# Moving three jobs along the steps of a two-layer banded-mixing kernel: inverse roots, output statistics, group norm

## The chip, the core and the metric

The kernel runs on one core of a Trainium2 chip. A core has a matrix engine (TensorE, PE in the profile; its weight loads are PEld), a vector engine (VectorE, DVE), a scalar engine (ScalarE, ACT), a general engine (GpSimd, POOL) and an engine that only issues transfers (SyncE, SP). Each works through its own list of instructions in order and waits for others by semaphores. The metric is the device time of one execution in microseconds (us); lower is better.

## The reference, cut to what matters

```python
for layer in (0, 1):                    # x: [1, 512, 512, 64] float32
    g  = _gn(x)                         # group norm: 32 groups of 2 channels over the whole picture
    xn = _ln(g, norm_scale, norm_bias)  # over the 64 channels of each pixel
    left  = (xn @ Wl + bl) * mask * sigmoid(xn @ Wlg + blg)    # 128 channels
    right = (xn @ Wr + br) * mask * sigmoid(xn @ Wrg + brg)
    gate  = sigmoid(xn @ Wog + bog)
    out = zeros
    for d in range(-4, 5):              # a band of nine rows
        out[i, j] += left[i, i + d] * right[i + d, j]
    out = _ln(out, out_norm_scale, out_norm_bias) * gate       # over the 128 channels
    x = x + out @ Wo + bo
```

The second layer's group norm needs the sums of the whole first layer, so the layers run one after the other.

## The kernel before

**Tiling.** The 512 rows are cut into nine blocks of 64 rows (they overlap by eight), the columns into two halves of 256 that lie on the two halves of the 128 partitions. A half has two chunks of `JC` = 128 columns, so a layer has 18 chunks; a chunk has `NU` = 16 units of `JU` = 8 columns. All arithmetic is float32.

**Steps.** `layer` runs over steps `t`. In step `t` unit `t` is projected, and output unit `t`, which was projected `LAG` = 30 steps earlier, is finished. So a layer has 288 steps with a projection, and 30 more that only finish outputs. In what follows "step 0" to "step 15" mean `t` modulo 16, and "step 12" is any `t` with that remainder. Instructions are put on each engine's list in the order in which the Python code emits them (`InOrder`), so the position in the loop body is the position in the queue, on SyncE's list too. The helper records every instruction as line 362, which is why the profile's rows all show L362 and have to be told apart by their tiles.

**A unit's way in.** Its pixels come by two DMAs from SyncE (`load`, z). Two steps later `affine` applies the group norm (z<-z,ga and z<-z,gb, on GpSimd; for the first units of a layer on VectorE). A step after that `inner_stats` takes four statistics instructions on VectorE (sti<-z). Every fourth step `solve` turns statistics into inverse roots. Then `inner_norm` (z<-z,sti and z<-z,rs, GpSimd), `transposed` (PE banks<-ident,z) and `kept` (ACT zT, and a DMA to `later`), and in the unit's own step two calls of `right`: PE projects (banks<-pack,zT), ACT takes the sigmoid (sg<-banks), and VectorE multiplies into RO (RO<-banks,sg).

**Mixing.** When the 16 units of a chunk are in RO, steps 0 to 9 of the next 16 run its 16 calls of `mix`, one or two a step (`2, 1, 2, 2, 1, 2, 1, 2, 2, 1`): 32 matmuls (banks<-RO,A), then one copy back to RO by ACT and one by VectorE.

**A unit's way out.** From step 10 on `out_stats` takes statistics of the mixed columns (sto<-RO, 64 instructions a chunk, four a unit). `solve` makes `rs` and `nm` of them. `norm(outs[t + 1])`, at the end of step `t`, is eight ACT instructions (on<-RO,nm,rs). In the next step follow `gates` (ACT gate<-bank), `turned` (PE bank<-ident,on, VectorE ZH<-bank,pack,gate), and `biased` (GpSimd XR<-XR), and one step later `end` (PE bank<-pack,ZH, VectorE XR<-bank,XR and two DMAs) and, in the first layer only, `sums` (PE acc<-XR).

**The inverse roots.** `solve` is five short VectorE instructions for a full set (var<-sti, var<-sto, var<-var, nm<-sto, rs<-var) followed by twelve on GpSimd, from rsqrt<-rs to nm<-nm,rs. Before the change it stands at the end of steps 3, 7, 11 and 15. The `affine` of step `t + 1` (`then_affine`) is put on GpSimd's list just ahead of it. The outputs whose statistics were complete at step 11 are first used by the `norm` at the end of step 13; those of steps 15, 3 and 7 by the `norm` at the end of steps 1, 5 and 9.

**PSUM.** `right`, `transposed` and `mix` share two buffers of two banks (banks); everything else turns in the single banks (bank). A projection can only start when the buffer two uses earlier was emptied.

Of the kernel before, what the change touches and what calls it, by code (L numbers as in the profile page):

```python
# [22 lines left out]
JU = 8  # L23
JQ = 4
NU = JC // JU
# [54 lines left out]
def tile_two_banded_layers(  # L80
# [7 lines left out]
    _, L, _, D = x.shape  # L88
# [326 lines left out]
    def affine(u: Unit, engine):  # L415

        engine.tensor_tensor(u.z, u.z, mid(ga, JU), ALU.mult)
        engine.tensor_tensor(u.z, u.z, mid(gb, JU), ALU.add)
# [57 lines left out]
    def right(u: Unit, q: int, w: dict):  # L476
        pr = projected(u, q, w["right"]).rearrange("p e k h -> p (e k) h")
        sg = wk.tile([P, JQ, H], F32, tag="sg", name="sg", bufs=2)
        en.scalar.activation(sg, pr[:, :, H:], AF.Sigmoid)
        en.vector.tensor_tensor(  # L480
            RO[:, :, u.c + q : u.c + q + JQ, :],
            pr[:, :, :H].rearrange("p j (h t) -> p h j t", t=2),
            sg.rearrange("p j (h t) -> p h j t", t=2), ALU.mult,
        )
# [31 lines left out]
    def take_left(n: int, h: int) -> bass.AP:  # L516


        A = lp.tile([P, S, HA], F32, tag="A", name="A")
        at = n * size + h * slab + WIN * HA  # L520
        for e in range(2):
            en.sync.dma_start(
                A[e * S : (e + 1) * S].rearrange("p i h -> p (i h)"),
                strided(left_of, at, ((S + 2 * WIN) * HA, S), (1, S * HA)),
            )
        return A
# [33 lines left out]
    def out_stats(o: Out, st: bass.AP, k: int):  # L560
        en.vector.bn_stats(
            st[:, k, :],
            RO[:, :, o.c + 2 * k : o.c + 2 * k + 2, :].rearrange("p h j t -> p h t j"),
        )
# [42 lines left out]
    def recall(o: Out):  # L607
        o.t = ztg.tile([P, JU // 2, P], F32, tag="zg", name="zg")
        en.sync.dma_start(o.t, later[o.at])
# [41 lines left out]
    def fetch(src: bass.AP, o: Out, w: dict, n: int):  # L651
        o.n, o.xr = n, XR[n % len(XR)]
        for e in range(2):
            en.sync.dma_start(o.xr[e * S : e * S + o.blk.m, :, 1 : 1 + 2 * D], rows_of(src, o, e))
# [38 lines left out]
    def layer(src: bass.AP, dst: bass.AP, w: dict, stats: bool, then=None):  # L693
        per = LH // JC
        n_chunks = len(blocks) * per
        LAG = NU + 14
        own = NU - JW // JU
        units, outs, lefts, mixes, looks, slabs = {}, {}, {}, {}, {}, {}
        free = NA * [NU - 2]
        for c in range(n_chunks):  # L700
            b, t0 = blocks[c // per], (c + 1) * NU
            for k in range(NU):
                t = c * NU + k
                units[t] = u = Unit(t, blk=b, j=c % per * JC + k * JU)
                j = k * JU if c % 2 == 0 else (JC + k * JU if k < own else JC - JW + (k - own) * JU)
                u.c = j

            for f in range(NU):
                o = outs[c * NU + LAG + f] = Out(
                    b, units[c * NU + (f + own) % NU], c % per * JC + f * JU  # L710
                )
                looks.setdefault(t0 + (8 + f if f > 3 else 10 + f // 2), []).append(o)

            step = [t0 + n for n, k in enumerate((2, 1, 2, 2, 1, 2, 1, 2, 2, 1)) for _ in range(k)]
            for n, t in enumerate(step):
                mixes.setdefault(t, []).append((c, n * HB))

            for h in range(H // HA):
                slabs.setdefault(free[-NA], []).append((c, h))
                free.append(step[(h + 1) * (HA // HB) - 1] + 1)  # L720
        for n in range(0, NEAR * JQ, JU):
            t = 3 + n // JU * 2
            lefts[t] = Unit(t, near=n)
        first_t, last_t = min(outs), max(outs)

        def inputs(t: int) -> list:
            return [d[t] for d in (units, lefts) if t in d]

        loads, affines, inners = {}, {}, {}
        count = [1, 1, 2, 1, 1, 1, 2, 1, 1, 1, 1, 0, 1, 1, 1, 0]
        ahead = {}
        done = -5 - NU
        for t in range(-7 - NU, n_chunks * NU):
            for _ in range(count[t % NU]):
                ahead[done + 7] = t
                done += 1
        for t in range(n_chunks * NU):
            for u in inputs(t):  # L740
                loads.setdefault(ahead[t] - 2, []).append(u)
                affines.setdefault(ahead[t], []).append(u)
                inners.setdefault(ahead[t] + 1, []).append((t, u))

        early = [u for t in sorted(loads) for u in loads[t] if u.near is None and u.at < 7]
        for u in early:
            load(src, u)
        yield
        A, sti, sto, then_affine = {}, {}, None, []
        for t in range(min(loads), last_t + 3):  # L750
            if then and t == max(units) + 2:
                then()
            for u in loads.get(t, []):
                if u not in early:
                    load(src, u)
            if t + 1 in outs:
                fetch(src, outs[t + 1], w, t + 1)
            for c, h in slabs.get(t, []):
                A[c, h] = take_left(c // per, h)
            if t + 2 in outs:  # L760
                recall(outs[t + 2])

            looking = []
            for o in looks.get(t, []):
                if sto is None:
                    sto = sm.tile([P, NB // 2, 6], F32, tag="sto", name="sto"), []
                st, os = sto
                n = len(os) * (JU // 2)
                looking += [(o, st[:, n : n + JU // 2, :], k) for k in range(JU // 2)]
                os.append(o)  # L770

            for v in looking[:3]:
                out_stats(*v)

            for u in affines.pop(t, []):
                affine(u, en.vector if u.at < NU + 4 else en.gpsimd)
            if t % 4 == 3 and t > NU:
                then_affine = affines.pop(t + 1, [])

            todo = []  # L780
            for at, u in inners.get(t, []):
                key = (at + 2) // 4
                if key not in sti:
                    sti[key] = sm.tile([P, 3 * NB // 4, 6], F32, tag="sti", name="sti", bufs=3), []
                st, us = sti[key]
                n = len(us) * (JU // 2)
                u.mean = st[:, n : n + JU // 2, 1::3]
                todo += [(u, st[:, n : n + JU // 2, :], k) for k in range(JU // 2)]
                us.append(u)

            if t in units:
                right(units[t], 0, w)
            for v in looking[3:5]:
                out_stats(*v)
            if t in outs:
                gates(outs[t], w)
            if t in units:
                right(units[t], JQ, w)
            if t in lefts:
                for q in range(0, min(JU, NEAR * JQ - lefts[t].near), JQ):  # L800
                    left(lefts[t], q, w)
            for u in inputs(t + 2):
                inner_norm(u)
            if t in outs:
                turned(outs[t], w)
            for u in inputs(t + 1):
                transposed(u)
                kept(u)
            if t in outs:
                biased(outs[t], w, stats)  # L810
            for v in looking[5:]:
                out_stats(*v)
            for v in todo:
                inner_stats(*v)
            if t - 1 in outs:
                end(dst, outs[t - 1], w)
            if stats and t - 2 in outs:
                sums(outs[t - 2], t - 2 == first_t, t - 2 == last_t)
            if t % 4 == 3:
                st, us = sti.pop((t + 5) // 4, (None, []))  # L820
                so, os = sto or (None, [])
                sto = None
                for u in then_affine:
                    affine(u, en.gpsimd)
                then_affine = []
                if us or os:
                    solve(w, us, os, st, so)
            if t + 1 in outs:
                norm(outs[t + 1])
            for n, (c, h0) in enumerate(mixes.get(t, [])):  # L830
                mix(c, A[c, h0 // HA], h0)
# [129 lines left out]
```

## Time and profile before

| | |
|---|---|
| median of three runs | 5036.04 us (5017.72 to 5038.81) |
| the profiled execution | 5033.71 us, span of its instructions 5031.9 us |
| engines' busy shares of the span | PE 84%, POOL 76%, DVE 77%, ACT 72% |
| mean granted TensorE clock | 0.963 |
| a chunk (16 steps) in the first layer, 1293.7 to 1415.5 | 121.80 us: PE 114.75, POOL 107.15, ACT 99.87, DVE 99.42 busy |
| 1293.7 to 1415.5: granted clock, DMA share | 1.00, 0.72 |

A row of the timeline gives start, duration, engine, line, operation, output<-inputs, shapes and how many instructions were merged; in brackets stands how long the engine had been idle just before and what released it. The row of a stretch gives its length, then for each engine its busy time and the number of instructions, the granted clock (1.00 is full speed), the DMA share and the rate. Four engines are each busy for more than four fifths of a chunk, so a mean tells little; the steps differ in what holds them.

### The profile page before, as it was taken

What the parts mean: (1) busy time and instruction counts of PE and PEld (TensorE: products, weight loads), DVE (VectorE), ACT (ScalarE), POOL (GpSimd) and SP (SyncE); (2) the same over time, 40 slices, a digit from 0 to 9 for tenths busy, and PEclk for the clock granted to TensorE, in tenths of its full rate; (3) what the DMA queues carried; (4) which work ended last, traced back from release to release, by engine and by line L of the source; (5) the groups of instructions that cost most, each with busy time, mean ns of one, the idle gap of its engine ahead of it and who ended that gap; (6) DMA issues with size and microseconds to landing.
All of it is one profiled execution on the core that took longest, in us unless ns stands there. A gap on an engine that the chain in (4) does not pass through costs nothing. (4 is left out here: it accounts for less than half of the span.)

```text
span 5031.9 us, 173294 instructions
## 1 busy us (share of the span) xinstructions
PE 4211.9 (84%) x67090; PEld 3564.2 (71%) x67090; DVE 3875.7 (77%) x9661; ACT 3636.6 (72%) x8156; POOL 3827.9 (76%) x4739
## 2 busy tenths in 40 slices
PE   1026899999999999999984589999999999998998
PEld 0024788888888888888863477777777777777776
DVE  6774778888888888888766478888888888888877
ACT  0013688888888888888883268888888888888888
POOL 0036888888888888888734688888888888888863
PEclk9988999999999999999997899999999999999999
DMA  7914677767776776777663457777777777777766
GB/s 316 406 57 120 172 200 200 204 197 200 203 199 199 198 201 198 198 199 205 190 168 95 118 172 199 203 202 201 199 205 201 202 202 202 204 204 202 206 186 173
DMA packets 905343, 982.32 MB, mean 195 GB/s; under 512 B 114210, under 2 KB 641608, under 8 KB 900168
## 3 DMA queue, kind: packets, MB, share of 16 engines
q1 hardware_dynamic: 897248, 948.49, 65.2%
q10 hardware_dynamic: 7272, 22.73, 1.1%
q8 instruction: 531, 8.70, 0.8%
q14 instruction: 292, 2.39, 0.2%
HBM read 658.42 MB, written 312.46 MB: 193 GB/s over the span
## 5 line engine op out<-in xcount | busy, mean ns | idle before, releaser
L362 ACT ACTIVATE on<-RO,nm,rs 128x128 f32<-128x128 f32 x4608 | 1868.6, 495 | 13.2 <-PE bank L362 12.7
L362 PE MATMUL banks<-pack,zT 64*128 64x256 f32 x9360 | 1322.6, 404 | 128.9 <-ACT zT L362 56.2
L362 PEld LDWEIGHTS banks<-pack,zT 64*128 64x128 f32 x9360 | 884.9, 194 | 493.7 <-DVE RO L362 200.8
L362 PE MATMUL banks<-RO,A 64*64 64x128 f32 x18432 | 1169.4, 279 | 14.4 <-ACT zT L362 14.4
L362 PEld LDWEIGHTS banks<-RO,A 64*64 64x64 f32 x18432 | 1097.4, 184 | 41.3 <-ACT zT L362 17.2
L362 DVE TENSOR_TENSOR RO<-banks,sg 128x512 f32<-128x512 f32 x1152 | 787.8, 684 | 347.6 <-ACT sg L362 331.5
L362 ACT ACTIVATE sg<-banks 128x512 f32<-128x512 f32 (+1 forms) x1188 | 694.7, 587 | 364.1 <-PE banks L362 254.3
L362 DVE COPY RO<-banks 128x512 f32<-128x512 f32 x576 | 397.9, 691 | 592.8 <-ACT RO L362 592.8
L362 DVE BATCH_NORM_STATS2 sto<-RO 128x6 f32<-128x256 f32 x2304 | 847.1, 414 | 1.2
L362 DVE SCALAR_TENSOR_TENSOR ZH<-bank,pack,gate 128x448 f32<-128x448 f32 (+1 forms) x1152 | 738.7, 683 | 51.3 <-ACT gate L362 39.5
L362 POOL TENSOR_TENSOR z<-z,gb 128x512 f32<-128x512 f32 x536 | 686.6, 1281 | 42.0
L362 PE MATMUL bank<-pack,ZH 128*64 128x64 f32 x18432 | 689.4, 230 | 5.6 <-ACT gate L362 5.2
L362 POOL TENSOR_TENSOR z<-z,ga 128x512 f32<-128x512 f32 x536 | 688.5, 1284 | 0.1
L362 POOL TENSOR_TENSOR z<-z,rs 128x512 f32<-128x512 f32 x586 | 616.1, 1051 | 46.0
L362 PEld LDWEIGHTS bank<-pack,ZH 128*64 128x64 f32 x18432 | 608.0, 142 | 47.8 <-ACT gate L362 9.2
L362 POOL TENSOR_TENSOR z<-z,sti 128x512 f32<-128x512 f32 x586 | 623.1, 1063 | 0.0
L362 ACT ACTIVATE gate<-bank 128x448 f32<-128x448 f32 (+1 forms) x1152 | 566.2, 544 | 73.1 <-PE bank L362 63.0
L362 PE MATMUL bank<-zg,pack 64*128 64x448 f32 (+1 forms) x2304 | 551.7, 550 | 1.2 <-DMA zg<-later 0.8
L362 ACT COPY RO<-banks 128x512 f32<-128x512 f32 x576 | 335.7, 583 | 299.2 <-PE banks L362 299.2
L362 PEld LDWEIGHTS bank<-ident,on 64*128 64x128 f32 x9216 | 402.6, 139 | 210.1 <-ACT gate L362 97.2
L362 POOL TENSOR_TENSOR XR<-XR,pack 120x512 f32<-120x512 f32 (+1 forms) x352 | 418.7, 1191 | 135.2 <-DMA XR<-in_x_dram 50.4
L362 PE MATMUL bank<-ident,on 64*128 64x64 f32 x9216 | 443.2, 225 | 86.3 <-ACT gate L362 59.3
(140 smaller groups left out, 3756.7 us busy)
## 6 DMA issues: line engine op xcount, KB each, us to landing
later<-zT SPq DMA_DIRECT2D x576, 256.0 KB
A<-left_of SPq DMA_DIRECT2D x576, 256.0 KB
zg<-later SPq DMA_DIRECT2D x576, 256.0 KB
z<-in_x_dram SPq DMA_DIRECT2D x576, 128.0 KB
z<-mid_x SPq DMA_DIRECT2D x576, 128.0 KB
gn_x<-in_x_dram SPq DMA_DIRECT2D x16, 4096.0 KB
XR<-in_x_dram SPq DMA_DIRECT2D x448, 112.0 KB
mid_x<-XR SPq DMA_DIRECT2D x448, 112.0 KB
```

The lines of the kernel that those rows point to most:

```text
L362: return lambda *a, **k: tc.keep_in_program_order(f(*a, **k))
```

## The change

1. **Inverse roots.** `solve` moves from steps 3, 7, 11, 15 to steps 4, 8, 12, 0 (`t % 4 == 0`), and with it the `affine` put ahead of it (now that of steps 1, 5, 9, 13). The sets are regrouped to fit: `key = (at + 1) // 4`. The step of each `norm` stays.
2. **Output statistics.** They are emitted one by one (an instruction takes two columns of each half) from a list of counts. Before: 8, 8, 4, 4, 4, 4 in steps 10 to 15, 4 in each of steps 0 to 7, none in 8 and 9. After: 5, 5, 6, 3, 3, 3 in steps 10 to 15, 7 in step 0, 4 in each of steps 1 to 8, none in 9. In a step the first three stand ahead of the first RO<-banks,sg, the fourth and fifth ahead of the second, the rest after ZH.
3. **Group norm.** The units handled in steps 0 to 15 were 1, 1, 2, 1, 1, 1, 2, 1, 1, 1, 1, 0, 1, 1, 1, 0 and become 1, 1, 2, 1, 2, 1, 1, 2, 1, 1, 1, 0, 1, 1, 0, 0. A unit's group norm then stands 7 to 10 steps ahead of its projection, where it was 7 to 9. Its two load DMAs stand two steps ahead of it, its statistics one step after it, and both move with it. In steps 0 to 15 of a layer's first chunk one unit is handled in each.

```diff
+        look = [n for n, k in zip(range(10, 25), (5, 5, 6, 3, 3, 3, 7) + 8 * (4,)) for _ in range(k)]
...
-                looks.setdefault(t0 + (8 + f if f > 3 else 10 + f // 2), []).append(o)
+                for k in range(JU // 2):
+                    looks.setdefault(t0 + look[f * (JU // 2) + k], []).append((o, k))
...
-        count = [1, 1, 2, 1, 1, 1, 2, 1, 1, 1, 1, 0, 1, 1, 1, 0]
+        count = [1, 1, 2, 1, 2, 1, 1, 2, 1, 1, 1, 0, 1, 1, 0, 0]
         ahead = {}
-        done = -5 - NU
+        done = -4 - NU
         for t in range(-7 - NU, n_chunks * NU):
-            for _ in range(count[t % NU]):
+            for _ in range(1 if 0 <= t < NU else count[t % NU]):
...
-            if t % 4 == 3 and t > NU:
+            if t % 4 == 0 and t > NU:
                 then_affine = affines.pop(t + 1, [])
...
-                key = (at + 2) // 4
+                key = (at + 1) // 4
...
-            if t % 4 == 3:
-                st, us = sti.pop((t + 5) // 4, (None, []))
+            if t % 4 == 0:
+                st, us = sti.pop((t + 4) // 4, (None, []))
```

No instruction is added or taken away; only their places in the queues change.

## The prediction

> **What bounds the kernel now.** I read the page first (PE 84%, no engine a clear bound), then the stretches of one chunk, then the timeline of each engine through one chunk of the first layer (1293 to 1500 us), because a chunk repeats almost exactly. Taking the first RO<-banks,sg of each step as its start, the median steps 0 to 15 over fourteen chunks last, in the first layer, 10.33, 7.16, 8.96, 8.97, 7.17, 8.97, 7.17, 8.44, 8.87, 7.72, 6.37, 7.01, 5.55, 5.69, 5.68, 8.81 us (122 in all); the second layer's steps differ by a few tenths and make 120.8.
>
> ```profile
> PE 4211.9 (84%) x67090; PEld 3564.2 (71%) x67090; DVE 3875.7 (77%) x9661; ACT 3636.6 (72%) x8156; POOL 3827.9 (76%) x4739
> ...
> 1411.20:1416.30 5.10, 1.86 (x26) 1.29 (x22) 5.07 (x11) 2.45 (x6) 4.50 (x7) 0.98 0.87 261
> 1416.30:1419.70 3.40, 3.37 (x58) 3.21 (x58) 2.67 (x5) 2.64 (x7) 2.80 (x9) 0.52 0.70 214
> 1425.90:1433.10 7.20, 7.20 (x128) 6.34 (x125) 5.89 (x16) 6.39 (x16) 6.96 (x7) 1.00 0.61 172
> ```
>
> The last row is a step 1: PE is busy for all of its 7.20 us. Steps 1 to 9 are PE's, and nothing in this change can shorten them. The first two rows are the seam at the end of step 15: PE works 1.86 of 5.10 us while DVE works 5.07, and afterwards the granted clock is 0.52 for 3.4 us.
>
> ```profile
> 1388.20 0.20 DVE L362 SCALAR_TENSOR_TENSOR var<-sto,pack 128x32 f32<-128x32 f32 x1
> 1388.65 0.20 DVE L362 TENSOR_SCALAR rs<-var 128x64 int32<-128x64 int32 x1
> ...
> 1411.18 0.72 DVE L362 TENSOR_SCALAR var<-sti 128x32 f32<-128x32 f32 x1
> 1411.82 1.31 DVE L362 SCALAR_TENSOR_TENSOR var<-sto,pack 128x32 f32<-128x32 f32 x1
> 1413.26 1.25 DVE L362 TENSOR_SCALAR nm<-sto 128x32 f32<-128x32 f32 x1
> 1415.52 0.67 DVE L362 TENSOR_TENSOR RO<-banks,sg 128x512 f32<-128x512 f32 x1
> ```
>
> ```profile
> 1416.33 0.69 PE L362 MATMUL banks<-ident,z 64*128 64x64 f32 x8 [2.83 <-POOL rsqrt L362]
> 1416.95 1.97 PE L362 MATMUL bank<-pack,ZH 128*64 128x64 f32 x32
> ...
> 1427.09 1.15 PE L362 MATMUL bank<-pack,ZH 128*64 128x64 f32 x32
> ```
>
> ```profile
> 1417.06 0.60 ACT L362 ACTIVATE zT<-banks 128x512 f32<-128x512 f32 x1 [3.41 <-PE banks L362]
> ```
>
> The five DVE instructions of `solve` take 0.73 us at step 11 and 3.4 at step 15 (1411.18 to 1414.61), where GpSimd's group norm runs. So the RO of step 0 starts at 1415.52, PE's transposes wait for that buffer (the profile names rsqrt, but it is RO at 1415.52 plus 0.67 that ends at 1416.19), and ACT stands 3.41 us. Steps 10 and 11 are DVE's: eight statistics of 0.33 us each. Steps 13 and 14 are ACT's, 5.69 us without a gap over 0.15.
>
> **The change part by part.** *Statistics, steps 10 to 12.* DVE's step at 10 is RO, RO, ZH x2, XR (2.95), 4 inner statistics (0.79) and 8 times 0.33: 6.37. With 5 it is 5.4, below ACT's 5.69. Steps 10, 11, 12 become 5.55, 5.69, 5.69 for 18.93: −2.0 us a chunk (second layer the same). The four statistics that go to step 8 lie in PE's time, as those of step 7 do now: 0; without that cover 1.3.
>
> *Roots out of step 15.* DVE then has 2.95 plus three statistics, 3.95, and the step is ACT's: 8.81 becomes 5.69, −3.1 (second layer 8.46 to 5.6, −2.9). *Step 0* keeps PE warm: ZH 1.97 to 1.15, acc 1.02 to 0.64, the z transposes 0.69 to 0.46. From 10.35 it comes to PE's 9.1, −1.25 (second layer 9.97 to 8.6, −1.4). DVE carries there seven statistics, no inner ones, and `solve`: done at RO+5.15, while the copies of `mix` come at RO+5.75, so it is covered by 0.6 us; what goes beyond that is PE's loss.
>
> *The new wait.* The `norm` of step 13 used roots of step 11; now it uses those of step 12.
>
> ```profile
> 1388.93 0.29 POOL L362 TENSOR_TENSOR rsqrt<-rs 128x64 f32<-128x64 f32 x1 [5.75 <-DVE rs L362]
> 1393.26 0.25 POOL L362 TENSOR_TENSOR nm<-nm,rs 128x32 f32<-128x32 f32 x1
> ...
> 1395.30 0.69 DVE L362 TENSOR_TENSOR RO<-banks,sg 128x512 f32<-128x512 f32 x1 [1.19 <-ACT sg L362]
> 1397.24 3.24 ACT L362 ACTIVATE on<-RO,nm,rs 128x128 f32<-128x128 f32 x8
> ```
>
> The twelve GpSimd instructions take 4.6 us (1388.93 to 1393.51), and `norm` starts 1.94 us after RO of step 13. After: DVE reaches `solve` at RO12+4.05 (2.95 and the three statistics that stand between), 0.73 for it, 4.6: roots at RO12+9.4. ACT wants them at 5.69+1.94 = 7.63. ACT stands 1.8 us, and behind it in its queue are the sigmoids that release RO of step 14, in ACT's own stretch: all of it counts.
>
> Is GpSimd free at that moment? A unit's group norm takes 2.63, its inner norm 2.13, XR 1.14. From the roots of step 8 (RO8+10.5) to those of 12 its list is 20.97: ready at RO8+31.5, DVE at RO8+31.55. They meet. Here a rule speaks against the change: the Trainium skill, "SBUF — State Buffer", section "SBUF: two separate sides", says that a DVE instruction in a two-port mode or with two SBUF inputs and a GpSimd instruction exclude each other for a whole instruction. The rows agree at step 15 (1.31 and 1.25, each as long as a group norm instruction) but show 0.20 at step 11, where GpSimd had run out of work. By the rule with full overlap I would add 2.7 at each such meeting, by the row of step 11 nothing; since the list ends just there, I take 0.2. The clock is the second place. PE would stand 0.44+2.0 = 2.45 us in step 13. "TensorE: Matmul & The Clock Gate", section "What's actually happening", gives about 3.4 us of idle time before the clock halves, so by it nothing. The trace has the half clock after 2.83, and after four gaps near 2.5 us twice. I take half of the 0.6 us by which slow transposes would delay zT: 0.3. Step 13: +2.3 (+2.6 in the second layer, where GpSimd comes 0.5 later). Between the ends 1.8 and 5.1.
>
> *Step 5.* Roots of step 4, not 3. From the roots of step 0 (RO0+9.8) GpSimd has 28.84 us of work, two group norms now in step 4: RO0+38.6, against DVE at 38.55. Roots at RO4+10.0.
>
> ```profile
> 1459.97 3.27 ACT L362 ACTIVATE on<-RO,nm,rs 128x128 f32<-128x128 f32 x8
> 1463.10 0.62 ACT L362 COPY RO<-banks 128x512 f32<-128x512 f32 x1
> ```
>
> That `norm` starts at RO4+8.99 (RO4 at 1450.98): 1.0 late, and the `mix` copy follows it without a gap, on whose buffer PE waits with 0.35 to spare: +0.65. In the second layer steps 0 to 3 are shorter, GpSimd is 1.0 late, `norm` 2.0: +2.0. *Steps 1 and 9:* roots of step 0 at RO0+9.8, wanted at 10.9: nothing; of step 8 at RO8+10.5, wanted at 10.6 (first layer) and 10.2 (second): +0.1 and +0.3. Before, these had 6 to 9 us to spare.
>
> *Group norm.* Same count; 16 in 16 steps. Its load DMAs move with it on SyncE (two a unit of about 0.55 us issue each). A load 12 steps ahead takes the buffer of the unit transposed the step before, behind whose zT store SyncE stands anyway: 0, and up to 1 us if not.
>
> *The tails.* In the 30 last steps of a layer ACT paces 4.03 us a step.
>
> ```profile
> 4967.62 1.01 ACT L362 ACTIVATE gate<-bank 128x480 f32<-128x480 f32 x2
> 4970.97 0.18 DVE L362 TENSOR_SCALAR rs<-var 128x32 int32<-128x32 int32 x1
> 4972.54 3.27 ACT L362 ACTIVATE on<-RO,nm,rs 128x128 f32<-128x128 f32 x8
> 4974.91 0.25 POOL L362 TENSOR_TENSOR nm<-nm,rs 128x32 f32<-128x32 f32 x1
> ```
>
> From the gate at 4967.62 to roots at 4975.16 are 7.55 us; the next step's `norm` comes after 4.92. A root one step later thus costs 2.65 at each of steps 12, 0, 4, 8, a little more with seven statistics, less where DVE held steps 10 and 11 before. About +13 in the last tail; +9 in the first, where a step takes 4.56. The start: the first roots wait for three more group norms and a set of statistics on DVE (about 5 us), against fewer loads bunched in step 0: +5 in all, between −10 and +15.
>
> Sum a chunk: first layer −2.0−3.1−1.25+2.3+0.65+0.1 = −3.3; second −2.0−2.9−1.4+2.6+2.0+0.3 = −1.4. Times 17 passes: −56 and −24; tails +22, start +5: −53. Against the profiled 5033.7: 4981. The median of the runs shown lies 2.3 above that execution, so 4983.
>
> **The rivals.** *A, GpSimd is behind at the meetings (slower).* Mechanism: at steps 4 and 12 DVE finds GpSimd still in its group norm, its five instructions take 3.4 instead of 0.73, and ACT's `norm` of steps 5 and 13 stands that much longer. For it: the list ends within 0.1 us of DVE in my working, and of a period of 119 us GpSimd has 113 of work plus 0.8 at four hand-overs. Against: the margin at steps 0 and 8 is over 1 us. Price: 4 us a chunk beyond what is counted, 34 passes, +136: 5119. It decides from 1.6 us a chunk on (53/34); below that the gain survives. *B, no measurable change:* the waits of `norm` eat the gain, with a cold PE at step 13 (0.6) and 2 us at step 5 in both layers: about 1.5 us a chunk more, 5034. *C, the wait at step 13 stays hidden:* then the first three terms alone count, −6.35 a chunk times 34, plus 27: 4847. For it, ACT could start late for another reason; against it, 9.4 against 7.63 with rows for both. *That the regrouping does nothing* I exclude: the places in the queues do change.
>
> **How the numbers follow.** About 0.5% (25 us) is what a measurement of this kernel can tell from no change. Likeliest case 0.44, its own range 4945 to 5020, of which 0.04 lies above 5011; C 0.10; B 0.22; A 0.24. Faster 0.50, same 0.26, slower 0.24. The range 4900 to 5105 leaves out most of C and the upper part of A.
>
> **What would show it.** Right: `solve` on DVE near 0.8 us at step 0; step 15 near 5.7 and step 0 near 9.1; the half clock gone from step 0; step 10 and 11 below 5.8; a new wait of ACT's on for POOL nm of about 2 us at step 13 and of 1 to 2 at step 5; in the tails waits of 2 to 3 us every fourth step. Wrong: on without a wait at step 13 (C); DVE's var and nm rows of 1.2 us at steps 4, 12 or 0 and PE gaps above 3 us (A).

## The result: 1.4% faster, and the profile after

| | before | after |
|---|---|---|
| median, run side by side | 5033.94 us (4 runs, 5017.72 to 5038.81) | 4959.99 us (4 runs, 4958.54 to 4963.24) |
| ratio | | 0.9856, 95% interval 0.9839 to 0.9874 |
| profiled execution | 5033.71 us, span 5031.9 us | 4958.54 us, span 4956.7 us |

The forecast was 4983 us with a range of 4900 to 5105. The time fell inside it, 23 us below the point.

From the page of the kernel before, the row of `norm` in the list of groups; then from the page of the kernel after, the engines' row and the row of `norm` (at its end: idle time of ACT ahead of it, and the releaser of most of it).

```profile
L362 ACT ACTIVATE on<-RO,nm,rs 128x128 f32<-128x128 f32 x4608 | 1868.6, 495 | 13.2 <-PE bank L362 12.7
```

```profile
PE 4181.7 (84%) x67090; PEld 3541.9 (71%) x67090; DVE 3844.0 (78%) x9661; ACT 3642.7 (73%) x8156; POOL 3820.6 (77%) x4739
...
L362 ACT ACTIVATE on<-RO,nm,rs 128x128 f32<-128x128 f32 x4608 | 1871.7, 495 | 128.4 <-POOL nm L362 108.4
```

The engines' row says nothing new: the counts are the same and the shares hardly move. The row of `norm` does. The releaser POOL nm does not occur in it before; now ACT loses 108.4 us to it. The change bought time and paid part of it back here.

**Where the time came from.** The step lengths are taken as in the prediction (first RO<-banks,sg of each step, medians over the fourteen chunks 4 to 17):

| step | 0 | 4 | 5 | 6 | 7 | 8 | 10 | 11 | 12 | 13 | 14 | 15 |
|---|---|---|---|---|---|---|---|---|---|---|---|---|
| layer 1 before | 10.33 | 7.17 | 8.97 | 7.17 | 8.44 | 8.87 | 6.37 | 7.01 | 5.55 | 5.69 | 5.68 | 8.81 |
| layer 1 after | 9.09 | 7.17 | 8.97 | 7.58 | 8.96 | 8.44 | 5.55 | 5.69 | 5.68 | 7.50 | 5.94 | 5.75 |
| layer 2 before | 9.97 | 7.49 | 8.50 | 7.26 | 8.19 | 8.51 | 6.37 | 7.02 | 5.56 | 5.88 | 5.57 | 8.46 |
| layer 2 after | 8.51 | 7.72 | 9.55 | 7.58 | 8.49 | 8.47 | 5.55 | 5.58 | 5.74 | 7.50 | 5.63 | 5.76 |

Steps 1 to 3 and 9 differ by 0.06 us at most. The layers divide like this (the tail runs from the first RO of step 287 to the last XR<-bank,XR of the layer; what lies ahead of a layer's first step is not in the table):

| stretch, us | layer 1 before | after | layer 2 before | after |
|---|---|---|---|---|
| first chunk | 149.7 | 131.4 | 146.2 | 130.0 |
| second chunk | 103.8 | 101.5 | 103.3 | 101.3 |
| chunks 3 to 17 together | 1833.1 | 1790.8 | 1811.4 | 1780.1 |
| last chunk (15 steps) | 111.9 | 113.3 | 110.4 | 111.7 |
| tail | 166.9 | 182.2 | 146.1 | 158.8 |

So 34.5 us come from the two first chunks and 73.6 from chunks 3 to 17 of both layers; the tails take back 28.0. With the second chunks (−4.3), the last chunks (+2.7) and what lies ahead of each layer's first step (+6.6), the sum is −75.1, against −75.2 between the spans. Where the text below speaks of a steady chunk, it is the mean of chunks 4 to 17.

**The seam is gone.** The row of each stretch: step 15, step 0 and step 1 of the same chunk as in the prediction. The columns are those of the stretches shown before: length, then busy time and number of instructions of PE, PEld, DVE, ACT and POOL, then the granted clock.

```profile
1376.40:1382.16 5.76, 5.31 (x95) 4.29 (x92) 4.15 (x8) 5.61 (x15) 5.05 (x5) 1.00 0.68 181
1382.16:1391.20 9.04, 8.60 (x154) 7.83 (x155) 7.30 (x19) 7.03 (x16) 6.83 (x13) 1.00 0.78 240
1391.20:1398.40 7.20, 7.20 (x128) 6.34 (x126) 5.88 (x15) 6.39 (x15) 6.89 (x9) 1.00 0.85 230
```

Where PE had worked 1.86 of 5.10 us at the end of step 15, it now works 5.31 of 5.76, and step 0 runs at full clock. The timeline of DVE in that step 0, then of PE:

```profile
1382.16 0.69 DVE L362 TENSOR_TENSOR RO<-banks,sg 128x512 f32<-128x512 f32 x1 [0.89 <-ACT sg L362]
...
1386.54 0.17 DVE L362 TENSOR_SCALAR var<-sti 128x32 f32<-128x32 f32 x1
1386.62 0.19 DVE L362 SCALAR_TENSOR_TENSOR var<-sto,pack 128x32 f32<-128x32 f32 x1
...
1387.06 0.20 DVE L362 TENSOR_SCALAR rs<-var 128x64 int32<-128x64 int32 x1
1387.86 0.69 DVE L362 COPY RO<-banks 128x512 f32<-128x512 f32 x1 [0.60 <-ACT RO L362]
```

```profile
1383.10 0.46 PE L362 MATMUL banks<-ident,z 64*128 64x64 f32 x8
1383.49 1.15 PE L362 MATMUL bank<-pack,ZH 128*64 128x64 f32 x32
```

`solve` takes 0.72 us (1386.54 to 1387.26) instead of 3.4, at RO+4.38, and 0.60 us of slack follow it, as worked out. PE's transposes take 0.46 and ZH 1.15, no longer 0.69 and 1.97.

**The new wait.** Steps 12 and 13 of the same chunk, each engine's timeline in turn. The first RO of step 12 is at 1357.62, that of step 13 at 1363.30.

```profile
1361.67 0.17 DVE L362 TENSOR_SCALAR var<-sti 128x32 f32<-128x32 f32 x1
...
1362.20 0.20 DVE L362 TENSOR_SCALAR rs<-var 128x64 int32<-128x64 int32 x1
```

```profile
1362.47 0.29 POOL L362 TENSOR_TENSOR rsqrt<-rs 128x64 f32<-128x64 f32 x1 [0.87 <-DVE rs L362]
...
1366.79 0.25 POOL L362 TENSOR_TENSOR nm<-nm,rs 128x32 f32<-128x32 f32 x1
```

```profile
1367.07 3.21 ACT L362 ACTIVATE on<-RO,nm,rs 128x128 f32<-128x128 f32 x8 [1.74 <-POOL nm L362]
```

The three fences are one chain across three engines: DVE makes rs until 1362.40, GpSimd's twelve instructions stand from 1362.47 to 1367.04, and ACT, idle for 1.74 us, starts 0.03 us later. The roots are thus ready at RO12+9.42, where the prediction had 9.4.

### The profile page after: what moved, and what is told of

It reads as the page before. It is cut to its first block, busy times and chain, and to the rows that moved or that the text cites. A ratio compares the mean times of both kernels' runs of the same rounds, so it can differ in the third digit from the quotient of the medians.

```text
span 4956.7 us, 173324 instructions
## 1 busy us (share of the span) xinstructions
PE 4181.7 (84%) x67090; PEld 3541.9 (71%) x67090; DVE 3844.0 (78%) x9661; ACT 3642.7 (73%) x8156; POOL 3820.6 (77%) x4739
## 3 DMA queue, kind: packets, MB, share of 16 engines
q14 instruction: 293, 2.39, 0.2%
## 4 chain that ended last, share of the span: by engine, by line
PE 53%; ACT 17%; DVE 12%; DMA 7%; POOL 4%; issue 3%; SPq 2%; ACTq 0%; another core or an unknown queue 0%; DVEq 0%; POOLq 0%
PE banks L362 29%; PE bank L362 21%; ACT on L362 11%; DVE RO L362 4%; SPq L362 2%; PE acc L362 2%; DMA left_of<-nothing 2%; POOL rsqrt L362 2%; DVE sti L362 2%; DVE ZH L362 2%; ACT RO L362 2%; ACT sg L362 2%; DVE XR L362 2%; ACT gate L362 1%; ACT zT L362 1%
## 5 line engine op out<-in xcount | busy, mean ns | idle before, releaser
L362 ACT ACTIVATE on<-RO,nm,rs 128x128 f32<-128x128 f32 x4608 | 1871.7, 495 | 128.4 <-POOL nm L362 108.4
L362 PE MATMUL banks<-RO,A 64*64 64x128 f32 x18432 | 1154.3, 277 | 12.7 <-ACT zT L362 12.7
L362 PEld LDWEIGHTS banks<-RO,A 64*64 64x64 f32 x18432 | 1082.3, 183 | 38.6 <-ACT zT L362 15.2
```

What stands on the lines that cost most here:

```text
L362: return lambda *a, **k: tc.keep_in_program_order(f(*a, **k))
```

## The experiments

Each was timed against the kernel before on the same chip. The first four shared one chip, where the kernel before had 5031.11 us, the last four another, where it had 5035.44. Kernels from different chips are set side by side by their ratios to it.

| kernel | us | ratio to before, 95% interval |
|---|---|---|
| rule only | 4994.28 | 0.9914 (0.9889 to 0.9939) |
| counts only | 4953.57 | 0.9839 (0.9820 to 0.9859) |
| roots and statistics only | 4977.53 | 0.9887 (0.9867 to 0.9907) |
| early roots | 4896.59 | 0.9726 (0.9706 to 0.9746) |
| before, group norm in its own step | 5029.43 | 0.9994 (0.9984 to 1.0005) |
| after, group norm in its own step | 4971.83 | 0.9878 (0.9855 to 0.9902) |
| shorter chain | 4828.37 | 0.9597 (0.9579 to 0.9616) |
| early roots and group norm | 4851.27 | 0.9644 (0.9623 to 0.9664) |

### Rule only: the first chunk

```diff
 # before
-            for _ in range(count[t % NU]):
+            for _ in range(1 if 0 <= t < NU else count[t % NU]):
```

> The kernel before with one thing of the change: in steps 0 to 15 of a layer's first chunk one unit's group norm is handled in each step. Theory 1 (the start's gain is this rule): the first chunk of each layer falls from 149.7 and 146.2 us to about 131 and 130, all later chunks keep 122.3 and 120.8, the tails keep 167 and 146; in all about 35 us less, near 5000. Rival (the start gained because the roots came later or the counts changed everywhere): the first chunks stay within 3 us and the time within 8 us of before, near 5034.

It is 0.9914, and the first chunks alone give it: they last 130.1 and 127.9 us where before had 149.7 and 146.2, while a steady chunk stays at 122.38 and 120.55 (122.27 and 120.75 before) and the tails at 166.4 and 145.7. All of the first chunks' gain in the full change is therefore this one line. Its first six steps show where: they last 3.5, 10.9, 13.4, 17.9, 7.0 and 21.1 us before, and 3.3, 8.0, 3.3, 16.6, 7.4 and 15.9 with the rule, 19.3 less in sum, half of it in step 2. SyncE's issues of z loads around that step, and VectorE's group norm that waits for one of them, first before (a row of SyncE runs from the first issue to the end of the last and takes in the time that it stood between them):

```profile
307.15 9.99 SPq L362 DMA_DIRECT2D z<-in_x_dram  x6
...
320.68 9.25 SPq L362 DMA_DIRECT2D z<-in_x_dram  x6
```

```profile
336.31 0.69 DVE L362 TENSOR_TENSOR z<-z,ga 128x512 f32<-128x512 f32 x1 [8.58 <-DMA z<-in_x_dram]
```

Then with the rule:

```profile
308.26 4.25 SPq L362 DMA_DIRECT2D z<-in_x_dram  x4
...
317.04 1.11 SPq L362 DMA_DIRECT2D z<-in_x_dram  x2
...
321.71 9.39 SPq L362 DMA_DIRECT2D z<-in_x_dram  x6
```

```profile
337.77 0.69 DVE L362 TENSOR_TENSOR z<-z,ga 128x512 f32<-128x512 f32 x1 [1.70 <-DMA z<-in_x_dram]
```

Before, the count of 2 in step 2 of the first chunk asks VectorE for a second unit whose load has only just been issued; VectorE stands 8.58 us for it with its RO products behind. With one unit a step that group norm comes a step later, and the stop that is left in this stretch is 1.70. The load itself comes no sooner: the waiting group norm is the layer's seventeenth in both kernels, and it starts 26.3 us behind the layer's first RO before and 26.7 with the rule. What changed is the order on VectorE: the first RO of step 3, which stood behind it, comes 27.8 us after the layer's first RO before and 14.6 with the rule. ACT gains as well: in the waits of the first chunk its sg stood 49.5 us for the left operand's transfers before and 33.6 with the rule.

### Counts only, and roots and statistics only: what cleared the seam

```diff
 # counts only: rule only, and
-        count = [1, 1, 2, 1, 1, 1, 2, 1, 1, 1, 1, 0, 1, 1, 1, 0]
+        count = [1, 1, 2, 1, 2, 1, 1, 2, 1, 1, 1, 0, 1, 1, 0, 0]
-        done = -5 - NU
+        done = -4 - NU
```

> The kernel before with the whole third part of the change (group norm counts, first-chunk rule), roots and output statistics as before. Theory 1 (the seam at step 15 is made by where the roots and statistics stand): beyond the start's 35 us the later chunks gain under 1 us each, near 5000, and the VectorE roots of step 15 still take about 3.4 us. Rival (the seam is made by GpSimd's group norm standing beside the roots; with none in steps 14 and 15 GpSimd is 2.6 us further ahead): the roots of step 15 take 0.8 to 2 us, steps 15 and 0 lose 2 to 4 us together, a chunk gains 2 to 4 us, near 4900 to 4930, which would be faster than the whole change.

```diff
 # roots and statistics only: after, with the count list, the loop line and done of before
-        count = [1, 1, 2, 1, 2, 1, 1, 2, 1, 1, 1, 0, 1, 1, 0, 0]
+        count = [1, 1, 2, 1, 1, 1, 2, 1, 1, 1, 1, 0, 1, 1, 1, 0]
-        done = -4 - NU
+        done = -5 - NU
-            for _ in range(1 if 0 <= t < NU else count[t % NU]):
+            for _ in range(count[t % NU]):
```

> The changed kernel with the old group norm counts and without the first-chunk rule: roots a step later and statistics spread, nothing else. Theory 1: the start's 35 us are lost again, the steady chunks keep most of their gain: GpSimd's list before the roots of step 0 is one group norm (2.63 us) longer than in the changed kernel, whose GpSimd stood 2.1 us there of which 0.8 is VectorE's own five instructions, so it is about 1.4 us late and costs 0.5 to 2 us a chunk at steps 0 and 1; near 5010 to 5050. Rival (the counts don't matter in the steady chunks): a chunk stays at 119.4 and 118.6 us, near 4995.

Either half clears most of the seam alone. With the counts only, a steady chunk is 120.71 and 119.20 us, although `solve` still stands at the end of step 15: step 14 has no group norm any more, and step 15 is 6.32 and 6.41 us, step 0 8.97 and 8.50. The timeline of DVE at that `solve`, then one row of GpSimd's, shows why not 5.7:

```profile
1387.07 0.17 DVE L362 TENSOR_SCALAR var<-sti 128x32 f32<-128x32 f32 x1
1387.16 0.20 DVE L362 SCALAR_TENSOR_TENSOR var<-sto,pack 128x32 f32<-128x32 f32 x1
1387.39 1.15 DVE L362 TENSOR_SCALAR var<-var 128x32 f32<-128x32 f32 x1
...
1388.58 0.20 DVE L362 TENSOR_SCALAR rs<-var 128x64 int32<-128x64 int32 x1
```

```profile
1387.24 1.27 POOL L362 TENSOR_TENSOR z<-z,gb 128x512 f32<-128x512 f32 x1
```

One of the five instructions still takes 1.15 us instead of 0.2: it ends at 1388.54, just behind GpSimd's z<-z,gb (1388.51). At step 3 two of them do (`solve` takes 2.53 us in the first layer), and that step grows there from 8.97 to 10.13. No `norm` waits, and the tails stay at 167.4 and 145.7.

With the roots and statistics only, a steady chunk is 119.43 and 117.60 us: in the first layer what the full change has (119.41), in the second one microsecond less than the full change's 118.62. The tails are 182.4 and 159.1, so they belong to the roots, not to the counts. The first chunks lose their gain (154.0 and 151.3).

So the gains of the halves overlap. Of a steady chunk's −2.9 and −2.1 us in the full change, the counts alone give −1.6 and −1.6, the roots and statistics alone −2.8 and −3.2. Once the roots are moved, the new list of counts thus gains nothing in a steady chunk; the old list with the line for the first chunk was not run. And since the counts alone keep the short tails, they reach 0.9839, no slower than the full change with 0.9856; the intervals overlap, so these two cannot be ranked.

### Early roots: is it really the wait at step 13?

```diff
 # after
+            early_roots = t % 4 == 0 and t > 2 * NU
+            if early_roots:                 # ahead of turned, not at the end of the step
+                for v in looking[5:]:
+                    out_stats(*v)
+                looking = []
+                roots(t)                    # sti.pop, solve
...
-            if t % 4 == 0:
-                st, us = sti.pop((t + 4) // 4, (None, []))
-                so, os = sto or (None, [])
-                sto = None
-                for u in then_affine:
-                    affine(u, en.gpsimd)
-                then_affine = []
-                if us or os:
-                    solve(w, us, os, st, so)
+            if t % 4 == 0 and not early_roots:
+                roots(t)
+            for u in then_affine:
+                affine(u, en.gpsimd)
+            then_affine = []
```

> The changed kernel; from the third chunk on, the inverse roots of steps 4, 8, 12, 0 are emitted ahead of ZH and XR in their step (after the step's last output statistics), and the group norm of the next step goes onto GpSimd's list behind them instead of ahead. Theory 1 (ACT's norm of steps 13 and 5 and of the tails waits for the roots, and VectorE's place in the step sets when they are ready): roots 1.8 us earlier in the step, so the wait at step 13 (1.74 us now) falls under 0.3, the one at step 5 (up to 1.7 in the second layer) under 0.3, the tails give back 20 to 28 us; about 3 us a chunk at step 13 and 5 in the second layer, 2.2 in the first: 34 chunks times 2 to 2.6 and the tails make 85 to 115 us less than the changed kernel, near 4850 to 4875. Rival (GpSimd's total work sets the pace, so its roots come no earlier): the waits stay, near 4960. Second rival (later ZH delays end and PE's single banks): steps 0, 4, 8 and 12 grow by 0.5 to 1.5 us each, near 4950 to 5000.

4896.59 us, 0.9726. The roots keep their step but start 1.8 us earlier in it (RO+2.28 at step 12, after has RO+4.05), ahead of ZH and XR on DVE and ahead of the group norm on GpSimd. The tails come back (167.8 and 147.7, before 166.9 and 146.1), step 13 falls from 7.50 to 5.78 and 5.77, and ACT's waits on nm fall from 108.4 us to 6.6. The steady chunks gain 1.14 and 1.30 us, less than the 1.7 at step 13, since step 14 grew to 6.85 (and step 4 of the second layer to 8.33). There the order that was given up asks its price; PE's timeline at step 14, then GpSimd's ahead of it:

```profile
1361.55 0.47 PE L362 MATMUL banks<-ident,z 64*128 64x64 f32 x8 [0.96 <-POOL z L362]
```

```profile
1355.38 0.25 POOL L362 TENSOR_TENSOR nm<-nm,rs 128x32 f32<-128x32 f32 x1
1356.74 1.28 POOL L362 TENSOR_TENSOR z<-z,ga 128x512 f32<-128x512 f32 x1
...
1360.45 1.04 POOL L362 TENSOR_TENSOR z<-z,rs 128x512 f32<-128x512 f32 x1
```

The group norm of step 13, now behind the roots, stands ahead of the inner norm whose result (z<-z,rs, until 1361.49) PE transposes next. PE waits 0.96 us for it.

### Group norm in its own step, from before and from after

```diff
 # before
-            if t % 4 == 3 and t > NU:
-                then_affine = affines.pop(t + 1, [])
 # after
-            if t % 4 == 0 and t > NU:
-                then_affine = affines.pop(t + 1, [])
```

The one on before:

> The kernel before with one edit: the group norm of the step after the roots stays in its own step instead of standing on GpSimd's list just ahead of the roots. Roots, statistics and counts as before. Theory 1 (step 15 is long because GpSimd's group norm stands beside VectorE's five root instructions, and the half clock of step 0 follows from that): the roots of step 15 take about 0.8 us instead of 3.4, step 15 falls from 8.8 to about 6.3, step 0 from 10.35 to about 9.0, a chunk gains 3 to 4 us, in all 100 to 135 us less, near 4900 to 4930; what could take it back is that group norm now stands ahead of the inner norm of the next step. Rival (the statistics and the place of the roots make the seam): step 15 stays above 8 us, near 5030.

5029.43 us, 0.9994: no difference, where the theory expected a gain. The seam did clear: step 15 falls from 8.81 to 6.99 and step 0 from 10.33 to 8.97 (second layer 8.46 to 7.00, 9.97 to 8.50), with DVE's `solve` at 1.52 instead of 3.4. Nothing else was touched, so most of the seam was a group norm of GpSimd beside VectorE's five short instructions. What is left of it is one of the five (var<-sti, 1.01 us from 1413.43), which now ends with GpSimd's XR<-XR (1413.22, 1.19 us). But step 13 grows from 5.69 to 7.68 (5.88 to 7.67), and a steady chunk stays at 121.91 and 120.63 (122.27 and 120.75 before). The timelines of step 12 to 13 on GpSimd, PE and ACT show what was traded:

```profile
1393.30 0.25 POOL L362 TENSOR_TENSOR nm<-nm,rs 128x32 f32<-128x32 f32 x1
1393.51 1.27 POOL L362 TENSOR_TENSOR z<-z,ga 128x512 f32<-128x512 f32 x1
1394.86 1.27 POOL L362 TENSOR_TENSOR z<-z,gb 128x512 f32<-128x512 f32 x1
...
1397.21 1.04 POOL L362 TENSOR_TENSOR z<-z,rs 128x512 f32<-128x512 f32 x1
```

```profile
1398.31 0.40 PE L362 MATMUL banks<-ident,z 64*128 64x64 f32 x6 [1.79 <-POOL z L362]
```

```profile
1398.82 0.60 ACT L362 ACTIVATE zT<-banks 128x512 f32<-128x512 f32 x1 [2.15 <-PE banks L362]
```

Behind the roots, the two group norm instructions (2.6 us) delay the inner norm, and with it transposes and zT. Placing it ahead of the roots had avoided just that. The expectation priced the wait removed and not the one that follows it.

The one on after:

> The changed kernel with the same edit: group norm of steps 1, 5, 9, 13 stays in its own step. Theory 1: the roots of step 4 in the second layer take 0.73 us instead of 1.72 and its step 5 falls by about 1 us, nothing else moves: 15 to 20 us less, near 4942. The wait at step 13 stays at 1.7 us, since VectorE's place sets it. Rival (the group norm behind the roots delays the inner norm and so PE's transposes of the next step): steps 2, 6, 10 or 14 grow by about 1 us, near 4980.

4971.83 us, 0.9878, by the ratios 11 us slower than the full change, though the intervals overlap. This theory fell: in the second layer `solve` at step 4 still takes 1.59 us (1.72 in after), step 5 stays at 9.55, and steps 14 and 15 grow to 6.27 and 6.69 (5.63 and 5.76). The rows of GpSimd and DVE at one such step 4 show why, first in after:

```profile
3176.42 1.27 POOL L362 TENSOR_TENSOR z<-z,gb 128x512 f32<-128x512 f32 x1
3176.60 1.12 DVE L362 TENSOR_SCALAR var<-sti 128x32 f32<-128x32 f32 x1
```

Then with the group norm in its own step:

```profile
3185.70 1.27 POOL L362 TENSOR_TENSOR XR<-XR,pack 120x512 f32<-120x512 f32 x1
3185.97 1.05 DVE L362 TENSOR_SCALAR var<-var 128x32 f32<-128x32 f32 x1
```

The group norm was what met DVE in after, as the theory had it; without it XR<-XR stands in its place, and another of the five instructions waits. With one unit in step 4 instead of two (roots and statistics only) GpSimd is ahead and `solve` takes 0.72 us there, but then it is 1.75 at step 0.

### Shorter chain: the wait by its length

```diff
 # after, in the Newton steps of the inverse roots
-        e.tensor_tensor(t, o, o, ALU.mult)
-        e.tensor_tensor(t, t, v, ALU.mult)
-        e.tensor_scalar(t, t, -27.0 / 1024.0, 0.5625, ALU.mult, ALU.add)
-        e.tensor_tensor(o, o, t, ALU.mult)
+        if e is nc.vector:
+            e.tensor_tensor(t, o, o, ALU.mult)
+            e.tensor_tensor(t, t, v, ALU.mult)
+            e.tensor_scalar(t, t, -27.0 / 1024.0, 0.5625, ALU.mult, ALU.add)
+            e.tensor_tensor(o, o, t, ALU.mult)
```

> The changed kernel without the second refinement of the inverse root on GpSimd (the last four of the ten instructions; the roots are less exact): 1.6 us less between VectorE's rs and the roots, at every fourth step. Theory 1 (ACT waits for the roots at steps 13 and 5 and in the tails): the wait at step 13 falls from 1.74 to about 0.15, the one at step 5 of the second layer to about 0.1, the tails lose about half of what they gained over before: 54 + 17 + 15, near 4875. Rival (ACT's wait covers something else that comes as late, PE or the reload of z): under 20 us less, near 4945.

4828.37 us, 0.9597. This kernel leaves out the second refinement on GpSimd, so its roots are less exact and it does not stand as a version of the program. With four instructions fewer on GpSimd the roots come 1.5 us sooner (RO12+7.92 for 9.42). Step 13 falls to 6.03 in both layers, step 5 of the second layer from 9.55 to 8.49, and the tails to 176.5 and 151.1. The row of `norm` in the waits (in us: total, times, longest; a line inserted above moved the helper to L363):

```profile
ACT on L363 <- POOL nm L363: 21.9, 41, 1.9
```

Of 108.4 us 21.9 are left. The rest of the gain is not the wait: GpSimd also has four times 1.5 = 6 us less to do in a chunk, and in the second layer step 4 (7.72 to 7.18) and step 6 (7.58 to 7.26) come down as well. This kernel therefore bounds what a shorter chain can give; it does not isolate it.

### Early roots and group norm: both prices off

```diff
 # early roots, and
-            for u in affines.pop(t, []):
-                affine(u, en.vector if u.at < NU + 4 else en.gpsimd)
-            if t % 4 == 0 and t > NU:
-                then_affine = affines.pop(t + 1, [])
+            if t % 4 != 1 or t <= 2 * NU:
+                for u in affines.pop(t, []):
+                    affine(u, en.vector if u.at < NU + 4 else en.gpsimd)
...
             # behind the inner_norm of the step
+            for u in affines.pop(t, []):
+                affine(u, en.gpsimd)
```

> The version with early roots, with the group norm of steps 1, 5, 9 and 13 (from the third chunk on) emitted in its own step behind that step's inner norm. In the run of early roots step 14 took 6.85 us: after the roots of step 12 GpSimd's list had XR (1.14), group norm (2.63) and then the inner norm (2.13), so that PE's transposes of step 14 came 1.2 us late. Theory 1: inner norm ahead of group norm takes that away, step 14 back to 5.7, and the group norm no longer stands beside the roots: 34 times 1.15 less, near 4857. Rival (step 14 was long for another reason, say a cold PE): step 14 stays near 6.8, near 4895.

4851.27 us (4847.43 to 4858.06), 0.9644: the fastest version that computes everything, by the ratios 2.2% below the full change. The roots go first, the inner norm second, the group norm last. ACT's timeline at step 13, then the row of `norm` in the waits:

```profile
1347.82 3.26 ACT L362 ACTIVATE on<-RO,nm,rs 128x128 f32<-128x128 f32 x8
```

```profile
ACT on L362 <- POOL nm L362: 6.4, 5, 1.9
```

The `norm` stands without a wait (its step's RO is at 1345.83, so it starts at RO+1.99, where the prediction puts an undisturbed one), step 14 is 5.69 and 5.58, and a chunk lasts 116.99 and 115.56 us. What is left is again DVE beside GpSimd: `solve` at step 4 takes 1.58 and 1.75 us, and in the second layer step 8 is 9.32. Moving one group norm from step 4 to 5 on top of this was not tried.

## Why the prediction was right, and where it missed

**Statistics, steps 10 to 12:** forecast −2.0 in both layers; measured −2.01 and −2.08. Right, and the cover in step 8 held (8.87 to 8.44).

**Step 15 and step 0:** forecast −3.1 and −1.25, in the second layer −2.9 and −1.4; measured −3.06 and −1.24, −2.70 and −1.46. The mechanism was right too: the kernel with the group norm in its own step cleared more than half of the seam by moving nothing else. What the prediction didn't see is that the counts would have taken most of it by themselves.

**The wait at step 13:** forecast +2.3 and +2.6 in steps 13 and 14; measured +2.07 and +1.68. The wait (1.74 in the row) was right to a tenth in the first layer. The half us of lateness that the second layer's GpSimd was given did not come: its nm ends at RO12+9.48, the first layer's at 9.42.

**Steps 5 and 9:** forecast at step 5 +0.65 and +2.0. The roots of step 4 were forecast at RO4+10.0 and came at 9.71 and 10.87, and `norm` waits 0.66 and 1.25 us where 1.0 and 2.0 were worked out. In the first layer step 5 itself does not change; step 6 grows by 0.41, and falls back to 7.17 in early roots, where no `norm` waits. (Step 7's +0.52 and step 8's −0.43 stay in that run, so they are not this delay.) In the second layer steps 4 to 8 are +1.86 together, step 5 alone +1.05. Step 9 has nothing to show.

**The rule weighed at step 12:** by the rule of the Trainium skill, "SBUF — State Buffer", section "SBUF: two separate sides", that one of the two engines stands for a whole instruction of the other, the prediction put a full meeting at 2.7 us (3.4 less 0.73), and took 0.2. At step 12 `solve` took 0.72 and 0.78 by the median, so there is next to no meeting there; at step 4 of the second layer it took 1.72, a partial one. Rival A is this mechanism; by the medians it happened in one place of eight, for 1 us. That it was not more is in part luck: in the chunk shown above GpSimd's list ends at 1361.60, 0.07 us before `solve` begins (the 0.87 us of idle time ahead of rsqrt say so), in most of the second layer's chunks it ends 0.2 us after, and in one chunk of each layer `solve` of step 12 took 1.99 and 2.43. The working had the two engines within 0.1 us, which is less than it can tell.

**Steady sum:** forecast −56 and −24 for 17 passes. Outside the first chunks the two layers moved by −43.2 and −32.0, in all −75 against −80. The first layer's gain was put too high and the second's too low, and these errors in part cancel. Two of the reasons are in the first layer's terms. The step lengths are medians, but the seam of before is not the same in each chunk: in six of fourteen step 15 took 7.6, not 8.8. By the means, steps 15 and 0 gain 3.6 us, not 4.3 (the medians of before add up to 122.9, a steady chunk is 122.3). And the last of the 17 passes has no step 15 to gain from: it is 1.4 us longer, not 3.3 shorter.

**Tails:** forecast +22, measured +28.0 (15.3 and 12.7). The last layer's is right (+13), the first layer's was put at 9. ACT's timeline in the last tail has the wait every fourth step, as said, at 2.5 to 3.2 us instead of 2.65:

```profile
4894.80 3.21 ACT L362 ACTIVATE on<-RO,nm,rs 128x128 f32<-128x128 f32 x8 [3.18 <-POOL nm L362]
...
4914.05 3.21 ACT L362 ACTIVATE on<-RO,nm,rs 128x128 f32<-128x128 f32 x8 [2.54 <-POOL nm L362]
...
4933.31 3.21 ACT L362 ACTIVATE on<-RO,nm,rs 128x128 f32<-128x128 f32 x8 [2.53 <-POOL nm L362]
```

**Start: the term that was mis-sized.** Forecast +5, between −10 and +15; measured −27.9: −34.5 in the first chunks, +6.6 ahead of them. The +6.6 is near the +5 that was said for later first roots, but these alone do not make it: roots and statistics only has +1.1 there, counts only +1.3, and what both together add was not traced. The loop line that leaves one unit a step in the first chunk was named ("fewer loads bunched in step 0") and not worked out, though the trace of before had the 8.58 us stop of DVE and SyncE's bunches of six loads to work it out from. This one term (33 us) is larger than the 23 us by which the sum was off; the tails (+6) and the steady sum (+5) fell the other way. That the point came so near is therefore in part luck; the terms for the seam, the statistics and the wait are not.

Rival C (no wait at step 13) is excluded by the row of 1.74 us; the early-roots kernels show that it was worth having. Rival B was half true: the waits of `norm` did come, at steps 13 and 5 and in the tails, but did not eat the gain.

## What to carry to other kernels

A short serial chain that crosses three engines (here 0.7 us on VectorE, 4.6 on GpSimd, then ScalarE) needs a step of distance between its end and its consumer, or a place early in its step: when it moves by a step it must be priced by when it ends, not by what it occupies. On an engine that serves two consumers, each position in its list decides a different wait, so when one is removed, ask which of the others takes its place; here roots first, inner norm second, group norm last was the fastest of the orders that were run. And price the first and the last pass on their own: one line that only acts in the first chunk gave nearly half of what this change brought (34.5 of 75.2 us).

## What the runs showed of the hardware that was not expected

**TensorE's clock halves after shorter gaps than expected, and not each time.** The kernel after has the half clock in step 14, in 7 of the 14 chunks of each layer. In the first layer it follows a gap of PE near 2.3 us, in the second two shorter ones (0.72 and 1.02 us in the chunk that has its step 14 at 3245.97). PE's timeline in two neighbouring chunks of the first layer:

```profile
1490.07 0.71 PE L362 MATMUL bank<-ident,on 64*128 64x64 f32 x15 [2.28 <-ACT gate L362]
...
1608.92 0.97 PE L362 MATMUL bank<-ident,on 64*128 64x64 f32 x15 [2.28 <-ACT gate L362]
```

The same gap of 2.28 us, and the second time the transposes behind it take 0.97 instead of 0.71 us, at a granted clock of 0.54 (stretch 1609.4 to 1612.8; 1.00 in 1490.0 to 1493.4). The Trainium skill, "TensorE: Matmul & The Clock Gate", section "What's actually happening", has about 3.4 us of idle time before the clock halves; there is no gap of that length in these chunks. The prediction took half of the price for it, and half of the chunks paid it.

In the trace the half clock of after always begins on one grid of 3.41 us. The rows of PE in the piece of this grid that holds most of the gap, in each of the two chunks (length, busy time and instructions, granted clock, DMA share and rate):

```profile
1486.27:1489.68 3.41, 1.52 (x13) 1.00 0.38 110
1605.74:1609.15 3.41, 1.13 (x15) 1.00 0.52 148
```

The second is the one that the half clock follows. In the first layer's fourteen chunks the seven with the half clock have PE busy for 1.13 to 1.40 us in the emptiest such piece around step 14, the seven others for 1.52 or more, with gaps of 2.26 to 2.39 us in all of them: where the gap falls in the grid seems to decide. In the second layer the two groups have 1.46 to 2.22 and 2.28 or more, so the limit is not one figure of busy time, and what it is stays open. Early roots and group norm, where that gap is gone, has no half clock in any of these chunks.

**VectorE stands when it comes second.** In chunks 4 to 17 of both layers, all ten kernels together, 474 of `solve`'s VectorE instructions took more than 0.4 us instead of 0.2, and every one of them ended within 0.1 us of the end of a GpSimd instruction of 512 columns (group norm, inner norm or XR<-XR). Another 134 overlapped such an instruction and kept their 0.2 us; all of these had started before it or at most 0.14 us after its start. So it is the order of the two starts that decides, and the wait is for the whole GpSimd instruction, as the rule weighed at step 12 has it. The statistics and the RO products in the same stretches are not touched: in before, after and counts only none took longer than 0.43 and 0.70 us.
